# RWKV layers of a four-layer sequence: lower halves of the values read from PSUM, mixed differences of decays and gates by ACT and GpSimd in groups two to four

## The chip, the core and the metric

The kernel runs on one core of one Trainium2 chip. The time is the device time of one execution in microseconds (us); shown is the median over several runs. The engines are named as in the profile: PE (matrix multiply; PEld its weight loads), DVE (VectorE), ACT (ScalarE), POOL (GpSimd) and SP (SyncE, which here only issues transfers). Each engine works through its own queue in order.

## What is computed

Four layers run one after another on x (16 sequences x 100 steps x 512 channels, f32), each with the context ctx (16 x 361 x 512): attention (layer 0), RWKV (1), attention with a feed-forward part (2), RWKV (3). The change lies in the RWKV layers. Their first half, cut to what matters:

```python
xa = _ln(x, ln1_w, ln1_b)
sx = jnp.concatenate([state[:, 1:2] - xa[:, :1], xa[:, :-1] - xa[:, 1:]], axis=1)
xxx = jnp.tanh((xa + sx * maa_x) @ maa_w1).reshape(b, l, 5, DM)
xxx = jnp.einsum('blfd,fde->blfe', xxx, maa_w2)
xm = xa[:, :, None] + sx[:, :, None] * (maa_stack + xxx)
xk, xw, xv, xr, xg = (xm[:, :, j] for j in range(5))
w = jnp.exp(-jnp.exp(time_decay + jnp.tanh(xw @ td_w1) @ td_w2))
r, k, v = xr @ Wr.T, xk @ Wk.T, xv @ Wv.T
g = jax.nn.silu(xg @ Wg.T)
def step(s, rkvw):
    a = k_t[..., :, None] * v_t[..., None, :]
    out = jnp.einsum('bhi,bhij->bhj', r_t, u * a + s)
    s = a + w_t[..., :, None] * s
```

The five mixed inputs are numbered f = 0 (k), 1 (decay w), 2 (v), 3 (r), 4 (gate g). Each is xa + sx * (stack_f + xxx_f); `sx` is the difference of neighbouring steps.

## The kernel before

Activations lie with channels on the 128 partitions. The 512 channels are 4 chunks (NC, index c or co), the 16 sequences 4 groups (NG) of 4 sequences (G), so that one tile is 128 channels x 400 steps (T). The groups are counted from one in the text and from zero in the code: g = 0 is group one.

`rwkv` is one loop over units u, written out at build time. From u = 0 on, a unit is one pair of the 16 value columns of a chunk: 8 units a chunk, 32 a group, 128 a layer. In each unit

- `spread(u + 1)`: PE copies two value columns over the partitions into one of two PSUM pairs, `vb`. It needs the pair free, that is the scan of unit u - 1 done;
- `product(u)`: DVE writes the first state (`vb<-s`) and multiplies with k in place (`vb<-vb,kc`);
- `scan(u)`: DVE runs two scans over time into `a`; POOL multiplies `a` with r;
- in odd units `gather`: PE sums earlier products of `a`, those of units u - 3 and u - 2, into the bank `acc`.

Around this stands, as pieces of PE work with a budget for each unit, all else: the projections of the next group (`projections(g, base)`), the output of the last one, the second half of the layer. Group one is projected before u = 0, when there are no scans; groups two to four while the scans of the group before them run. The order on every engine is fixed at build time: `pin`, `mm` (L94), `turn` (L97) and the `InOrder` wrapper (L89) keep program order, so most operations show the line of the wrapper and are told apart by tile names.

The pieces use three PSUM banks in turn (`Slots`). `bank()` gives the next one, passes over one that a projection holds half done, and first emits the reader that still waits for it. `read_later` emits a reader at the end of the next unit, or as soon as its bank is asked for, or when a consumer calls it.

For one group `projections` runs through these stages:

1. layer norm, transposes, `sx`, the low-rank part `inner`;
2. the mixing stage: `repeated((0, 1))` and `mixed((0, 1), c)`, with `repeated((2, 3))` after the first chunk; for each f and chunk a matmul into a bank, then `read(f, ps)`. It writes a tile `tm` (a ring of 4, shared with others): DVE adds the column `stack{f}` to PSUM and multiplies with `sx`, POOL adds `xa` into `xj[f]`. `decay_in` follows, two matmuls for each chunk (`td_w` on xj[1], `maa_w` on xm), and first calls all readers of f = 1;
3. f = 2 and 3 with the projections k (`Wk`), and `repeated((4,))`;
4. the value stage, for each chunk c: the projection v (`plain(2, "Wv", "v", c)`), `decay(c)` (matmul with `td2`, two exponentials on ACT: `ew`, `wd`) and `mixed((4,), c)`;
5. r (`Wr`), and later the gates (`Wg`).

`plain` copies a projection on ACT into a stage tile (a ring of 6) and stores it to DRAM. For v it calls `split`: ACT rounds the bank into `hi` (the float32r upper half); DVE subtracts, `lo = v - hi`, where `v` is the stage copy in SBUF. `low` is handed to `slots.read_later` with the bank `ps`, though it reads only SBUF tiles; `enter` calls what is left of it for a chunk's loads. `hi` is stored from ACT's queue, `lo` from SP's. Both are read back for `spread`.

Of the kernel before, what the change touches and what calls it, by code (L numbers as in the profile page):

```python
# [10 lines left out]
F32R = mybir.dt.float32r  # L11
BF16 = mybir.dt.bfloat16
U8 = mybir.dt.uint8
AF = mybir.ActivationFunctionType
ALU = mybir.AluOpType
# [6 lines left out]
T = G * L  # L22
# [15 lines left out]
def xattn_sequence(ctx: ExitStack, tc: tile.TileContext, d: dict, out: bass.AP):  # L38
# [52 lines left out]
    vector, scalar, gpsimd = InOrder(nc.vector), InOrder(nc.scalar), InOrder(nc.gpsimd)  # L91

    def mm(**kw):
        pin(nc.tensor.matmul(**kw))  # L94
# [606 lines left out]
    def rwkv(n, ws, small, first, next_weights, last):  # L701
# [6 lines left out]
        with ExitStack() as es:  # L708
# [9 lines left out]
            vec, w1, td1, gwb = (small[k] for k in ("vec", "w1", "td1", "gwb"))  # L718
# [205 lines left out]
            def projections(g, base):  # L924
# [6 lines left out]
                def store(t, c, tile):  # L931
                    (nc.sync if t in ("lo", "g") else scalar).dma_start(out=to[t][c], in_=tile)

                rows = [xb[g * G + i] for i in range(G)]
                st, xn, xj = {}, [], {}
# [85 lines left out]
                def mixed(fs, c):  # L1021

                    banks = []
                    for f in fs:
                        if c == 0:
                            xj[f] = two.tile([128, NC, T], F32, tag="xm", bufs=4, name=f"xj_{nm}_{f}")
                        banks.append(slots.bank())
                    for f, ps in zip(fs, banks):
                        cols = slice(c * 128, (c + 1) * 128)
                        mm(out=ps[:, :T], lhsT=w2[f][:, cols], rhs=zs[f], start=True, stop=True)  # L1030

                    def read(f, ps):
                        tm = two.tile([128, T], F32, tag="tm", bufs=4, name=f"tm_{nm}_{f}_{c}")
                        vector.scalar_tensor_tensor(
                            tm, ps[:, :T], vec[f"stack{f}"][:, c : c + 1], st["sx"][:, c, :], ALU.add, ALU.mult
                        )
                        gpsimd.tensor_tensor(steps(xj[f][:, c, :]), steps(tm), xa(c), ALU.add)

                    for f, ps in zip(fs, banks):
                        mixes[f].append(slots.read_later(ps, lambda f=f, ps=ps: read(f, ps)))  # L1040

                def linear(f, w, co, read, tag):

                    before = mixes[f] if f >= 0 else soon
                    x = lambda c: xj[f][:, c, :] if f >= 0 else st["xm"][:, c, :]
                    chain(2.7, late, tag, before, lambda ps: ps[:, :T],
                          lambda c: w[:, c, co * 128 : (co + 1) * 128], x, read)
# [3 lines left out]
                def plain(f, w, t, co):  # L1051
                    def read(ps):
                        out = stage(f"{t}_{nm}_{co}")
                        scalar.copy(out[:, :T], ps[:, :T])
                        store(t, co, out[:, :T])
                        if t == "v":
                            split(ps, out[:, :T])

                    def split(ps, v):

                        hi = stage(f"hi_{nm}_{co}")[:, :T]
                        scalar.copy(hi.bitcast(F32R), ps[:, :T])
                        store("hi", co, hi)

                        lo = stage(f"lo_{nm}_{co}")[:, :T]

                        def low():
                            vector.tensor_tensor(lo.bitcast(F32R), v, hi, ALU.subtract)
                            store("lo", co, lo)

                        lows[co] = slots.read_later(ps, low)

                    linear(f, ws[w], co, read, ("in", g, co if t == "r" else 0))
# [362 lines left out]
            while u < UNITS + 6 or pieces or slots.due or slots.late:  # L1436
# [23 lines left out]
                elif short and len(put) == NG and blended < NG:  # L1460
                    g = blended
# [485 lines left out]
```

## Time and profile before

| | |
|---|---|
| median of 3 runs | 3131.18 us (3127.56 to 3131.5) |
| the profiled execution | 3127.86 us, of it a span of 3126.1 us |
| PE, busy share of the span | 2858.8 us, 91% |
| DVE | 1675.5 us, 54% |
| ACT | 1308.6 us, 42% |
| POOL | 1159.3 us, 37% |
| mean granted PE clock | 0.961 |
| POOL `a<-a,rc` | 256 x 1908 ns |
| DVE scans `a<-wc,vb` | 512 x 974 ns |
| POOL `xj<-tm,ext` | 160 x 981 ns |
| DVE `tm` | 160 x 625 ns (median) |
| DVE `lo` | 32, median 612 ns, sum 37.35 us |

The first RWKV layer is at work from about 690 to 1345 us of the span, the second from about 2440 us to the end. In the first, group one's values are made at 724 to 746 us, group two's at 829 to 862, group three's at 962 to 990 and group four's at 1088 to 1114; their mixing stages for f = 0 and 1 lie at 694 to 706, 788 to 807, 902 to 921 and 1030 to 1047. The second layer repeats this about 1754 us later.

The profile's views are read so. A group of instructions has a line, an engine and an operation, `out<-in` by the program's names, shapes, count, busy time, mean duration and the idle time in front of it with its releaser. A row of waits reads: engine and tile, `<-` whom it waited for, us in total, times, longest. A timeline row reads: start, length, engine, line, operation, `xcount`, and in brackets the idle time before it and the releaser; rows with a count above one are merged. A window row gives for each engine the busy time in it. Ends of matmuls are modelled, and POOL spans are rough.

### The profile page before, as it was taken

How to read it: one execution, taken by the hardware profiler on the slowest of the kernel's cores; microseconds unless marked ns; L12 is line 12 of the kernel's file. 1: busy time of each engine (PE TensorE's matmuls, PEld its weight loads, DVE VectorE, ACT ScalarE, POOL GpSimd, SP SyncE). 2: the span in 40 equal slices, each digit the busy share in tenths (PEclk: the TensorE clock that was granted, in tenths of full speed). 3: DMA queues.
4: the chain of work that ended last, by engine and by line, in shares of the span. 5: the costliest groups of instructions: out<-in, count | busy, mean ns of one | idle time of the engine just before them, and what ended most of it. 6: DMA issues, size and time to landing. Idle time of an engine off the chain costs nothing. (4 is left out here: it accounts for less than half of the span.)

```text
span 3126.1 us, 44079 instructions
## 1 busy us (share of the span) xinstructions
PE 2858.8 (91%) x16323; PEld 1488.0 (48%) x16323; DVE 1675.5 (54%) x3507; ACT 1308.6 (42%) x2921; POOL 1159.3 (37%) x953
## 2 busy tenths in 40 slices
PE   6999999878889999989999999989999789999998
PEld 3555555534344444444555555455555344444444
DVE  2555556553989988433333333331000369998981
ACT  3777677753435355422222232221111335344553
POOL 0111111133777777412222111220000367787771
PEclk9999999989999999989999999999999889999999
DMA  6010101013224353230000001020002323324321
GB/s 196 24 34 24 34 24 37 3 39 116 80 77 129 96 161 87 71 88 21 21 22 21 21 21 34 28 71 11 11 11 62 101 63 106 109 76 155 105 60 56
DMA packets 139561, 195.93 MB, mean 63 GB/s; under 512 B 23974, under 2 KB 106854, under 8 KB 139346
## 3 DMA queue, kind: packets, MB, share of 16 engines
q1 hardware_dynamic: 116306, 160.34, 17.3%
q10 hardware_dynamic: 23040, 32.78, 2.9%
q8 instruction: 128, 2.10, 0.3%
q14 instruction: 87, 0.71, 0.1%
HBM read 117.16 MB, written 49.15 MB: 53 GB/s over the span
## 5 line engine op out<-in xcount | busy, mean ns | idle before, releaser
L89 POOL TENSOR_TENSOR a<-a,rc 128x800 f32<-128x800 f32 x256 | 487.8, 1908 | 175.8 <-DVE a L89 113.1
L89 DVE TENSOR_TENSOR_SCAN a<-wc,vb 128x400 f32<-128x400 f32 x512 | 477.4, 974 | 28.1 <-PE acc L94 2.2
L89 DVE CUSTOM_DVE_ANT_0 pr<-l_sc,mask 100x361 f32<-100x361 f32 x512 | 252.1, 529 | 148.7 <-PE l_sc L94 148.6
L89 ACT ACTIVATE pr<-pr,nm 100x361 f32<-100x361 f32 x512 | 301.2, 593 | 5.8 <-POOL sums L89 3.7
L89 DVE TENSOR_TENSOR vb<-vb,kc 128x792 f32<-128x792 f32 x256 | 253.8, 991 | 8.8
L97 PEld LDWEIGHTS l_pT<-ident,pr 100*121 100x121 f32 x1536 | 193.3, 186 | 104.3 <-issue 50.9
L1639 DVE CUSTOM_DVE_ANT_0 junk<-l2a_sc,mask 100x361 f32<-100x361 f32 x256 | 136.9, 535 | 182.5 <-PE l2a_sc L94 165.0
L94 PE MATMUL vb<-xc,sel 128*128 128x400 f32 x512 | 207.0, 487 | 18.0 <-DVE a L89 17.8
L97 PE MATMUL l_pT<-ident,pr 100*121 100x100 f32 x1536 | 216.4, 276 | 6.2 <-ACT pt L89 4.3
L1675 POOL TENSOR_TENSOR pa<-pt,pt 121x1600 f32<-121x1600 f32 x16 | 57.1, 3570 | 363.7 <-ACT pt L1670 363.7
L89 ACT COPY pt<-l_pT 121x400 f32<-121x400 f32 x256 | 125.1, 489 | 149.5 <-PE l_pT L97 148.5
L1860 DVE TENSOR_TENSOR x<-pb,x 100x512 f32<-100x512 f32 x16 | 12.6, 790 | 319.9 <-DMA pb<-po 310.1
L89 POOL TENSOR_TENSOR xj<-tm,ext 128x400 f32<-128x400 f32 x160 | 153.6, 981 | 80.1 <-DVE tm L89 59.8
L94 PE MATMUL v<-l_v_w,ct 128*121 128x512 f32 x384 | 177.0, 605 | 0.0
L75 PE MATMUL h<-yTb,l_fc 128*128 128x400 f32 x512 | 172.8, 499 | 0.6 <-ACT yTb L343 0.6
L94 PE MATMUL k<-ct,l_k_w 128*128 128x361 f32 x512 | 170.6, 476 | 0.0
L75 PE MATMUL p<-l_proj,h 128*128 128x512 f32 x384 | 165.5, 592 | 0.0
L89 POOL TENSOR_SCALAR ve<-mv 100x1 f32<-100x1 f32 x16 | 3.6, 224 | 409.8 <-DVE mv L89 409.8
L94 PEld LDWEIGHTS vb<-xc,sel 128*128 128x128 f32 x512 | 97.2, 198 | 109.5 <-issue 36.1
L94 PE MATMUL l_sc<-kz,qz 32*100 32x361 f32 x1024 | 112.6, 509 | 36.1 <-DVE nm L89 33.9
L89 DVE COPY pt<-l_pT 121x400 f32<-121x400 f32 x128 | 73.5, 574 | 132.1 <-PE l_pT L97 64.8
L75 PEld LDWEIGHTS h<-yTb,l_fc 128*128 128x128 f32 x512 | 96.9, 190 | 74.3 <-ACT yTb L343 2.5
(298 smaller groups left out, 5158.0 us busy)
## 6 DMA issues: line engine op xcount, KB each, us to landing
ct<-in_ctxT SPq DMA_DIRECT2D x32, 722.0 KB
dk<-k ACTq DMA_DIRECT2D x32, 200.0 KB
kc<-dk SPq DMA_DIRECT2D x32, 200.0 KB
dv<-v ACTq DMA_DIRECT2D x32, 200.0 KB
dhi<-hi ACTq DMA_DIRECT2D x32, 200.0 KB
dlo<-lo SPq DMA_DIRECT2D x32, 200.0 KB
vc<-dv SPq DMA_DIRECT2D x32, 200.0 KB
dw<-wd ACTq DMA_DIRECT2D x32, 200.0 KB
```

The lines of the kernel that those rows point to most:

```text
L75: nc.tensor.matmul(out=ps, lhsT=lhs(c), rhs=rhs(c), start=(c == 0), stop=(c == n - 1))
L89: return lambda *args, **kw: tc.keep_in_program_order(op(*args, **kw))
L94: pin(nc.tensor.matmul(**kw))
L97: pin(nc.tensor.transpose(out, in_, ident))
L1639: nc.vector.tensor_tensor_reduce(out=junk, in0=ss[r][:L, :S2], in1=t["mask"], scale=-1.0, scalar=FLT_MAX, op0=ALU.add, op1=ALU.min, accum_ ...
L1675: nc.gpsimd.tensor_tensor(t["pa"], t["pt"][0], pt, ALU.add)
L1860: nc.vector.tensor_tensor(x, pb[:, i, :], x, ALU.add)
```

## The change

`read` in `mixed` splits by f and group. For f = 1 and f = 4, in groups two to four (`g` not zero), ACT adds the column to the PSUM bank and writes `tm`, POOL multiplies `tm` with `sx` in place, and POOL's add of `xa` follows as before. All other f, and all of group one, stay with DVE. There are 4 chunks x 2 f x 3 groups x 2 layers = 48 such reads of 160.

`split` no longer gets the copy `v`. DVE computes `lo` from the bank itself, 32 times, in all groups.

```diff
                     def read(f, ps):
                         tm = two.tile([128, T], F32, tag="tm", bufs=4, name=f"tm_{nm}_{f}_{c}")
-                        vector.scalar_tensor_tensor(
-                            tm, ps[:, :T], vec[f"stack{f}"][:, c : c + 1], st["sx"][:, c, :], ALU.add, ALU.mult
-                        )
+                        if f in (1, 4) and g:
+                            scalar.activation(tm, ps[:, :T], AF.Identity, bias=vec[f"stack{f}"][:, c : c + 1], scale=1.0)
+                            gpsimd.tensor_tensor(tm, tm, st["sx"][:, c, :], ALU.mult)
+                        else:
+                            vector.scalar_tensor_tensor(
+                                tm, ps[:, :T], vec[f"stack{f}"][:, c : c + 1], st["sx"][:, c, :], ALU.add, ALU.mult
+                            )
                         gpsimd.tensor_tensor(steps(xj[f][:, c, :]), steps(tm), xa(c), ALU.add)
...
                         if t == "v":
-                            split(ps, out[:, :T])
+                            split(ps)
-                    def split(ps, v):
+                    def split(ps):
...
                         def low():
-                            vector.tensor_tensor(lo.bitcast(F32R), v, hi, ALU.subtract)
+                            vector.tensor_tensor(lo.bitcast(F32R), ps[:, :T], hi, ALU.subtract)
                             store("lo", co, lo)
```

No buffer, bank or piece is added, and PE's order is the same.

## The prediction

> **What bounds the kernel now.** The page first: PE is busy 91% of the span, DVE 54%, and in the two RWKV layers (690 to 1345 us and 2440 to 3126 us) both are near full. I then asked for the first RWKV layer in stretches cut by stage. Columns: length, then busy us of PE, PEld, DVE, ACT, POOL with instruction counts, granted clock, DMA.
>
> ```profile
> 755.00:828.00 73.00, 60.71 (x240) 29.49 (x238) 57.34 (x85) 23.32 (x40) 51.10 (x42) 0.86 0.21 60
> 828.00:866.00 38.00, 32.87 (x128) 15.36 (x124) 36.80 (x45) 24.38 (x47) 27.89 (x22) 1.00 0.41 134
> 962.00:996.00 34.00, 31.41 (x124) 14.78 (x122) 31.48 (x43) 24.65 (x48) 24.21 (x19) 1.00 0.53 170
> 1026.00:1060.00 34.00, 29.97 (x118) 13.73 (x116) 30.84 (x48) 9.91 (x17) 26.82 (x21) 0.80 0.26 73
> ```
>
> Rows 2 and 3 are where groups two and three make their values (Wv): DVE 97% and 93%, PE 86% and 92%. Row 4 is the mixed-difference stage of group four (row 1 holds group two's): POOL already 79%, and a clock below 1. No engine alone sets the pace: the chain of waits over 2500 to 2960 us has PE's mm at 34.4%, DVE's scans and products at 20.3%, DVE tm at 2.5%, DVE lo at 1.3%. So work taken off DVE pays only where DVE is last. Next, the two tiles that the change touches, and PE's waits over the whole run (us, times, longest):
>
> ```profile
> L89 DVE TENSOR_TENSOR lo<-v,hi x32: 549/612/3915, 728.1 to 2867.2; 128x400 fp32r<-128x400 f32 x32
> L89 DVE SCALAR_TENSOR_TENSOR tm<-mm,vec,sx x160: 607/625/635, 697.8 to 2863.7; 128x400 f32<-128x400 f32 x160
> L89 DVE TENSOR_TENSOR rk<-mm,vc x32: 548/549/575, 773.4 to 3013.4; 128x400 f32<-128x400 f32 x32
> ...
> PE mm L94 <- DVE tm L89: 18.7, 26, 1.8
> PE mm L94 <- ACT hi L89: 11.4, 13, 2.3
> PE mm L94 <- POOL xj L89: 4.5, 5, 1.4
> ```
>
> lo, with both inputs in SBUF, stretches up to 3915 ns; tm and rk, with one input in PSUM, never stretch. In the timeline the long ones lie over POOL's products:
>
> ```profile
> 859.11 3.92 DVE L89 TENSOR_TENSOR lo<-v,hi 128x400 fp32r<-128x400 f32 x1
> 859.72 1.88 POOL L89 TENSOR_TENSOR a<-a,rc 128x800 f32<-128x800 f32 x1
> ```
>
> **Part 1: lo from PSUM.** The 32 lo take 37.35 us (four windows, 2.30 + 16.25 + 2.30 + 16.50). At rk's 0.549 us, the same shape with PSUM and SBUF inputs, they take 17.6: 19.8 us less DVE work, nearly all in groups two and three. The PSUM row (549) is no slower than the quickest lo from SBUF (549), so I charge nothing for the source.
>
> [...]
>
> The move also adds a wait. lo now reads the PSUM bank, so PE's next matmul there waits for DVE's lo, not only for ACT's hi. With three banks taken in turn, the next taker is the next Wv group or the decay/gate mixing matmul before it. Group one shows the plainest case:
>
> ```profile
> 728.12 0.58 DVE L89 TENSOR_TENSOR lo<-v,hi 128x400 fp32r<-128x400 f32 x1 [6.21 <-ACT hi L89]
> 728.14 2.95 PE L94 MATMUL mm<-xj,l_Wv 128*128 128x400 f32 x8 [0.23 <-ACT hi L89]
> ```
>
> PE starts as hi ends; afterwards it starts after lo, 0.58 later, four times a layer (728, 733, 740, 745) with DVE idle: at most 2.3 us, and half of that where PE would have waited for ACT's ew anyway. I take +1.2 a layer.
>
> In groups two to four I walked the rows bank by bank. At 836.57 the mixing matmul follows hi (835.82); afterwards it waits for the scan (ends 837.13), rk (0.55) and lo (0.55): 838.2, 1.6 late, and behind it in PE's queue stand Wv (0.85 late) and a spread whose product is a unit off. At 857.94 Wr takes the bank of the last value: it must wait for the scan's end (859.19) and lo, about 2 us. Against this DVE gains 3.35 us on the lo at 859 and 0.62 on each tm. Both advances meet: DVE often catches up with ACT's hi and then waits for it, ACT in turn for the late PE. By the walk PE is 1.1 us ahead at 870 (group two, where "PE waits for DVE rk" shrinks), 0.2 ahead at 996, 0.2 behind at 1118: -1.1 a layer.
>
> **Part 2: tm of decays (f = 1) and gates (f = 4).** 4 chunks x 2 x 3 groups x 2 layers = 48. DVE loses 48 x 0.625 = 30 us. ACT gains 48 x about 0.59 (the row of ew, an activation with a bias from PSUM) = 28 us; ACT is busy 10 to 24 us of 34 to 38 in these stages, so this is hidden, except where its queue holds two table loads (845.4 to 848.6) ahead of a gate's tm: there decay's bank, freed by DVE at 848.7, comes about 1 us later. That is in the walk. Cover gone, it would be 48 x 0.59. POOL gains 48 multiplies; none of this shape on tm exists, but its flat 128x400 product (rk, 1.04 us) is the same form: 50 us, half in the mixing stage, where four multiplies come within three units. What is queued behind them: POOL's own adds to xj, then the next product a, for which PE's gather waits.
>
> The stage of group four shows the queue:
>
> ```profile
> 1041.19 1.88 POOL L89 TENSOR_TENSOR a<-a,rc 128x800 f32<-128x800 f32 x1 [0.43 <-DVE a L89]
> 1043.03 2.80 POOL L89 TENSOR_TENSOR xj<-tm,ext 128x400 f32<-128x400 f32 x3
> 1045.88 0.55 PE L94 MATMUL mm<-xj,td_w 128*64 128x400 f32 x1 [0.35 <-POOL xj L89]
> 1047.37 0.17 DVE L89 COPY vb<-s 128x8 f32<-128x8 f32 x1 [1.67 <-PE vb L94]
> ```
>
> POOL goes almost without a pause from 1036.1, and PE's decay matmul already waits for its last add. With two more multiplies by 1041.8 (one ahead of a, 0.6 late) and two among the three adds, that add ends near 1048.6: +2.75 us, and DVE behind it is waiting for PE already, so nothing hides it. Group two (POOL busy 791 to 802, PE waiting at 799.56) comes out 0.9 late; group three, whose decay chunk three starts 2.4 us after its add, 0.8. Together +4.4 a layer. Bounds: 0 if the earlier release of banks by ACT pays for it all, 4 x 1.04 = 4.2 in each of three groups (12.5) if none hides.
>
> **Sum.** A layer: +1.2 - 1.1 + 4.4 = +4.5; two layers +9.0. On the profiled execution (3127.86 us, a span of 3126.1 and 1.8 around it) this gives 3136.9. That execution lies 3.3 below the median of the runs (3131.18), and the forecast for the median is 3131.2 + 9, rounded to 3140.
>
> Ends: if only the gains reach the end, the chain gives them: its three lo in 2500 to 2960 us (0.89 + 3.84 + 1.13 = 5.86) shrink to 1.65, and tm's 2.5% of 460 us, 24/80 of it, is 3.5: -7.7 a layer, -15. If POOL hides nothing: 2 x (12.5 + 2.3) = +30.
>
> The clock is a further unknown. At 905 to 919 us it fell to half after PE gaps of at most 1.4 us, and matmuls of td_w took 0.87 to 0.93 instead of 0.50. So new waits of 1 to 2.75 us could cost clock too: 12 us at half clock hold 6 us of lost work. Equally, banks freed earlier could end a slow stretch sooner by as much. I take 0.
>
> [...]
>
> **Rivals.** *Faster, -15 (3116).* DVE's relief (50 us of 875 us in all stages of the two layers that hold the change) reaches the end. It decides if lo is done by the time PE returns to its bank, that is if DVE stays ahead of ACT's hi, and if PE's bank waits on tm (18.7 us, of which f = 1 and 4 own 30% by count) go too. For it: DVE at 97% and 93% in the value stages. Against: there PE is fed by hi from ACT, and the bank waits come back as lo.
> *No change, within 6.* Gains and the POOL tail cancel, as all waits are 1 to 2 us in a loop where three engines wait in turn. For it: my sum is a difference of such terms.
> *Much slower, +30 (3161).* POOL becomes the bound in the mixing stages, with the full multiplies exposed in six of them. For it: 79% busy in 1026 to 1060, 91% with four more. Against: the stage ends within 10 us and POOL then has pauses of 2 to 3 us (1050.64 came after 2.88 idle).
> That lo stays stretched is unlikely: no operation with a PSUM input stretched.
>
> **How the numbers follow.** Forecast (slower, +4 to +20, own range 3135 to 3151): 0.44; much slower 0.08; no change 0.16; faster 0.32. 0.2% is 6.3 us, about what a measurement of this kernel tells from no change; slower by more 0.50, within 0.18, faster 0.32, a little of the forecast's lower edge counted as within. The range 3113 to 3156 takes in the faster case and leaves out most of the much slower one.
>
> **What will show it.** Right: lo at 0.55 everywhere; DVE busy down by some 50 us, POOL up by as much; a new PE wait on lo of 8 us or more, PE's wait on POOL xj above 4.5; decay matmuls of group four some 2.7 us later within their stage. Wrong: if PE waits on lo stay under 3 us and the value stages shorten by 2 us or more each, the faster case holds; if PEclk in the mixing stages rises from 0.80 and 0.86 towards 1, the clock has paid, which I put at nothing.

## The result, and the profile after

The changed kernel takes 3159.81 us (median of 6 runs, 3153.92 to 3166.76), beside 3130.31 us (6 runs, 3125.14 to 3132.42) of the kernel before on the same chip: a ratio of 1.0099, 95% interval [1.0085, 1.0114], that is +31 us [+27, +36]. The forecast of +9 us had the direction; the time lies outside its range.

From here on, costs in us are (ratio - 1) times the median of the kernel before in the same series, with the interval worked out likewise. The expectations below sometimes give the difference of two medians instead (29.5 for the whole change, 15.1 for the decays alone).

The profiled execution took 3153.92 us, of it a span of 3152.1. The page's first part, busy time of each engine:

```profile
PE 2862.7 (91%) x16323; PEld 1493.6 (47%) x16323; DVE 1633.1 (52%) x3459; ACT 1334.6 (42%) x2969; POOL 1205.4 (38%) x1001
```

DVE lost 42 us of work, ACT got 26, POOL 46: the work moved as meant. The changed operations, by tile (shortest, median and longest duration in ns):

```profile
L89 DVE TENSOR_TENSOR lo<-mm,hi x32: 549/575/576, 725.7 to 2894.3; 128x400 fp32r<-128x400 f32 x32
...
L89 ACT ACTIVATE tm<-mm,vec x48: 573/594/610, 792.6 to 2891.0; 128x400 f32<-128x400 f32 x48
L89 POOL TENSOR_TENSOR tm<-tm,sx x48: 1024/1034/1049, 794.4 to 2894.8; 128x400 f32<-128x400 f32 x48
```

No lo stretches any more, and the prices taken from other rows (0.55, 0.59 and 1.04 us) hold within 0.03. What went wrong is not there but in what waits for these operations. PE's waits, the same view as before (total, times, longest):

```profile
PE mm L94 <- DVE lo L89: 27.9, 24, 2.5
PE mm L94 <- POOL xj L89: 26.2, 15, 3.8
...
PE mm L94 <- ACT tm L89: 12.2, 11, 1.5
...
PE mm L94 <- DVE tm L89: 6.2, 12, 0.8
```

PE stands 27.9 us at banks for lo, where it stood 11.4 for hi, and 26.2 instead of 4.5 us for POOL's xj.

To see where the time was lost, one DVE operation served as a mark: the 32 starts of rk, one for each chunk of scans. Marks 0, 4 and 8 of a layer stand ahead of the mixing stages of groups two, three and four, and the next mark behind each. The table gives how much each stretch between marks grew against the kernel before, in both layers: "mixing stages" sums the stretches 0 to 1, 4 to 5 and 8 to 9, "value stages" the rest up to the next group (1 to 4, 5 to 8, 9 to 12). (The expectations call such marks anchors and cut the stages a little differently.)

| kernel | against before, us | mixing stages | value stages |
|---|---|---|---|
| whole change | +31.0 [26.6, 35.7] | +17.7 | +7.7 |
| lo alone | +6.3 [2.5, 9.7] | +1.3 | +2.8 |
| tm alone (f = 1 and 4) | +19.4 [15.3, 23.5] | +18.2 | +2.9 |
| decays alone (f = 1) | +16.3 [11.3, 21.3] | +18.5 | -7.6 |
| gates alone (f = 4) | +4.4 [0.6, 7.8] | -1.3 | +5.9 |
| lo and gates | +14.4 [9.1, 19.7] | -0.2 | +17.6 |
| POOL's multiplies alone | +13.5 [9.4, 17.5] | +15.5 | -1.6 |
| decays, PE's waits filled | +5.3 [2.5, 8.1] | +11.9 | -4.6 |
| whole change, waits filled | +22.2 [16.9, 27.5] | +11.5 | +7.6 |
| before, two waits filled | +2.5 [-1.3, 5.9] | +3.0 | -2.0 |
| gates of group two alone | -3.4 [-7.8, 0.6] | +0.9 | +8.3 |

The last two columns come from one execution each, and executions of one kernel differ by 10 us and more (3121.61 to 3135.02 for the kernel before in one series). The last two kernels of the table, which take the time of the kernel before, show what that does. In the mixing stages they differ from it by 3 us at most, so that column can be read. In the value stages they differ by -2.0 and +8.3 us. The execution of before that serves as the yardstick was slow in one of these stages (group two, second layer: every kernel of the table came out 1.1 to 5.3 us shorter). And the last kernel leaves group three as it was, yet its stretches grew by 3.9 and 2.8 us in the two layers. So what stands firm is that whatever moves the decays loses 15 to 18 us in the mixing stages (12 with the waits filled). In the value stages only the +17.6 of lo and gates stands out; for the rest the times of the kernels decide, and that lo and the gates cost there follows from where their operations stand.

### The profile page after: what moved, and what is told of

It is laid out like the page before. It is cut to its first block, busy times and chain, and to the rows that moved or that the text cites. A ratio compares the mean times of both kernels' runs of the same rounds, so it can differ in the third digit from the quotient of the medians.

```text
span 3152.1 us, 44127 instructions
## 1 busy us (share of the span) xinstructions
PE 2862.7 (91%) x16323; PEld 1493.6 (47%) x16323; DVE 1633.1 (52%) x3459; ACT 1334.6 (42%) x2969; POOL 1205.4 (38%) x1001
```

## The experiments

**The parts one by one.** Four kernels: lo from PSUM with every tm on DVE; tm as changed with `lo = v - hi`; and the latter for one f only.

```diff
-                        if f in (1, 4) and g:
+                        if f == 1 and g:      # decays alone; f == 4: gates alone
...
-                            vector.tensor_tensor(lo.bitcast(F32R), ps[:, :T], hi, ALU.subtract)
+                            vector.tensor_tensor(lo.bitcast(F32R), v, hi, ALU.subtract)
```

> Part 1 alone: lo read from PSUM, every tm left with DVE. The whole change cost 29.5 us, by anchors in the trace about half in the mixing stages of f = 0 and 1 (+1.0, +2.3, +3.7 a layer) and half in the value stages (+1.5, +4.9, 0). Theory A (two causes: POOL's queue in the mixing stages, and in the value stages the gate's tm behind ACT's table loads, which makes hi and lo late): this kernel costs little, 0 to +5 us, and the mixing stages do not move. Rival B (PE waiting at its banks for lo is the main cost): +15 us or more. Rival C (the lo from PSUM gains what it saves of DVE, 20 us of busy time): -5 us or less. PE's waits on lo stay above 8 us in sum under A and B.

> Part 2 alone: tm of f = 1 and 4 in groups two to four by ACT and POOL, lo = v - hi from SBUF as before. Theory A: +20 to +30 us, nearly all of the change's cost. Rival B (lo's bank wait is the main cost): +5 to +14 us, the mixing stages' share alone. Rival C: as much as or more than the whole change (29.5 us), because lo stretches again over more POOL work.

> Only the decays' tm (f = 1) by ACT and POOL in groups two to four, the gates' tm with DVE, lo from SBUF. Theory A: +12 to +16 us (two layers times the +7.0 that the anchors show in the mixing stages), with PE's waits on POOL xj near 20 us. Rival (the mixing stage's delay is caught up in the stage behind it, where PE waits for DVE): within 5 us of before. Rival B and C make no statement of it.

> Only the gates' tm (f = 4) by ACT and POOL in groups two to four, the decays' tm with DVE, lo from SBUF. Theory A: +8 to +14 us, all in the value stages, with ACT's tm behind the loads of its tables and hi, lo and Wr late. Rival B: within 3 us of before, because without lo's wait at the bank ACT's lateness is hidden.

Measured: +6.3, +19.4, +16.3 and +4.4 us. The decays carry half of the change, and lo alone, which was meant to gain, costs too (PE waits 33.4 us for it). Theory A holds for the decays, is within the interval for lo (0 to +5 forecast) and puts the gates too high (+8 to +14); rivals B (lo above 15) and C (lo gains) fall. The parts add up to 27.0 us, and the intervals don't tell that from 31.0.

**Why the decays are dear: POOL, ACT or the ring?** First, DVE keeps tm, and POOL gets the same extra multiply into xj, which its add then overwrites:

```diff
+                        if f == 1 and g:
+                            gpsimd.tensor_tensor(xj[f][:, c, :], tm, st["sx"][:, c, :], ALU.mult)
                         gpsimd.tensor_tensor(steps(xj[f][:, c, :]), steps(tm), xa(c), ALU.add)
```

> The kernel before, with one more POOL multiply of 128x400 for each tm of f = 1 in groups two to four (tm times sx, written to xj, where POOL's add overwrites it), ahead of that add; DVE makes tm as before. It adds the POOL work of the decays' multiplies alone. Theory A (POOL's queue ahead of the last add): +12 to +18 us, PE's wait on xj near 25 us in sum. Rival C (ACT's part of the chain): within 5 us of before.

Measured: +13.5 us. Nothing else was changed, so POOL's work alone brings most of the decays' 16.3. PE's wait for xj in this run:

```profile
PE mm L94 <- POOL xj L89: 19.5, 10, 3.2
```

Second, all three steps in place in xj, without a tile of the ring:

```diff
-                            scalar.activation(tm, ps[:, :T], AF.Identity, bias=..., scale=1.0)
+                            tm = xj[f][:, c, :]
+                            scalar.activation(tm, ps[:, :T], AF.Identity, bias=..., scale=1.0)
```

> f = 1 by ACT and POOL in groups two to four as in the run with the decays alone, but all three steps work in place in xj, so that ACT needs no tile of the tm ring. In that run ACT waited for POOL's xj to give back a tm tile 4 times, 8.2 us, in the first RWKV layer. Theory A (POOL's work itself): +11 to +18 us, as with the ring. Rival (the ring: ACT held up, hence the bank, hence PE): +6 us or less.

Measured: +13.5 us [9.4, 17.8]; the ring is not it. Third, ACT adds the column in the bank and DVE multiplies:

```diff
+                            scalar.activation(ps[:, :T], ps[:, :T], AF.Identity, bias=..., scale=1.0)
+                            vector.tensor_tensor(tm, ps[:, :T], st["sx"][:, c, :], ALU.mult)
```

> For f = 1 in groups two to four ACT adds the column in place in the PSUM bank and DVE multiplies the bank with sx into tm; POOL has its add alone, as before. It adds the ACT operation and its latency without the POOL work. Theory A: -2 to +5 us, PE's wait on xj under 8 us. Rival C (ACT late as the first reader of the bank): +10 us or more.

Measured: +8.1 us [4.4, 12.2], between the two. Here the bank comes free only after ACT and DVE in turn, which neither kernel has: PE's wait for DVE's tm rose from 18.7 to 26.5 us, that for xj was 7.0 (4.5 before). It says that an ACT step put in front has a price of its own; it does not split the 16.3. Fourth, DVE makes the last add in POOL's place:

```diff
+                            gpsimd.tensor_tensor(tm, tm, st["sx"][:, c, :], ALU.mult)
+                            vector.tensor_tensor(steps(xj[f][:, c, :]), steps(tm), xa(c), ALU.add)
```

> f = 1 in groups two to four: ACT adds the column, POOL multiplies with sx, and DVE adds xa into xj. POOL has one operation for each chunk as in the kernel before, DVE one too; only who does which is exchanged, and the chain from bank to xj has the same three links as in the run with the decays alone (+15.1 us). Theory A (the amount of POOL work in the mixing stage): 0 to +7 us, PE's wait for POOL on xj gone. Rival C (the longer chain ACT, POOL, third operation is late, whoever does it): +12 us or more. DVE's add has both inputs in SBUF and may stretch over POOL's products, which would put some of it back.

Measured: +54.8 us [49.7, 60.1], far above what theory A allows; rival C's "+12 or more" takes in the number, but not by a late chain for PE, whose wait for POOL's xj fell to 2.0 us. The cost is not in DVE's add (median 0.575 us) but in DVE's queue: DVE waited 64.0 us, 22 times, for POOL's tm with the scans behind it. As a test of POOL's load it fails; it shows what a consumer of POOL costs on the engine that paces the scans.

**The clock behind the waits.** In the run with the decays alone, PE's timeline in the mixing stage of group three, second layer, reads (start, length, idle time before and its releaser):

```profile
2676.98 0.55 PE L94 MATMUL mm<-xj,td_w 128*64 128x400 f32 x1 [1.86 <-POOL xj L89]
...
2679.93 0.93 PE L94 MATMUL mm<-xj,td_w 128*64 128x400 f32 x1 [2.05 <-POOL xj L89]
...
2680.64 0.87 PE L94 MATMUL mm<-xj,td_w 128*64 128x400 f32 x1
...
2683.81 5.28 PE L94 MATMUL mm<-xj,l_Wk 128*128 128x400 f32 x8
```

After the second wait everything takes nearly twice as long: td_w 0.93 instead of 0.55, eight Wk 5.28 instead of 2.85. So PE was kept busy in these waits, in groups three and four, by matmuls with a zero weight that add zero to the bank:

```diff
                         for c in (2 * i, 2 * i + 1):
+                            for _ in range({2: (0, 2, 2, 2), 3: (0, 0, 4, 2)}.get(g, (0, 0, 0, 0))[c]):
+                                mm(out=ps[:64, :T], lhsT=zero, rhs=st["xm"][:, c, :], start=False, stop=False)
```

> The decays alone by ACT and POOL (+15.1 us), and in groups three and four PE gets matmuls with a zero weight (100 lines less than the waits: 6 a group, each about 0.67 us by the rows of td_w) in front of the decay matmuls that wait for POOL's xj; they add zero to the bank. If the half clock that follows those waits (td_w 0.93 and 0.87 instead of 0.50, Wk x8 5.28 instead of 2.85 us in the second layer's group three) is a part of the cost: the rows behind the filled waits run at 0.50 and 2.85, and the time falls to +6 to +12 us. Rival (the clock is only a companion, POOL's queue sets the time): +15 us within 3, whether the clock stays or not.

(The first parenthesis should say that the six a group are a little shorter than the waits.) The same stage then reads:

```profile
2672.21 0.55 PE L94 MATMUL mm<-xj,td_w 128*64 128x400 f32 x1 [0.36 <-POOL xj L89]
...
2675.16 0.55 PE L94 MATMUL mm<-xj,td_w 128*64 128x400 f32 x1 [0.72 <-POOL xj L89]
...
2677.83 2.85 PE L94 MATMUL mm<-xj,l_Wk 128*128 128x400 f32 x8
```

Measured: +5.3 us [2.5, 8.1] instead of +16.3 [11.3, 21.3]. PE's idle waits for xj fell from 26.0 to 10.4 us, but the 24 zero matmuls take some 24 x 0.67 = 16 (0.67 by the rows of td_w): PE is held up at POOL's xj about as long as in the run with the decays alone, partly at work for nothing. Still 11 us, give or take 6, are gone, and td_w and Wk are back at 0.55 and 2.85 us, with a granted clock of 0.90 instead of 0.74 in this stage (2657 to 2688 us): these 11 us were the clock. With the fill in the whole change:

> The whole change, with PE's zero-weight matmuls in front of the waiting decay matmuls of groups three and four as in the run with the decays alone and filled waits (which came to +5 us instead of +15). If the half clock behind the POOL waits carries 10 us of the cost, whatever else is changed: +18 to +22 us against before. Rival (the other parts of the change take up what the clock gives): +27 us or more. Second rival (the mixing stages were the root of the value stages' loss too): +15 us or less.

Measured: +22.2 us instead of +31.0; the intervals overlap, but the 9 us agree with the 11, and the marks show the gain where the fill stands (mixing stages +17.7 to +11.5).

The kernel before has half clock too (0.51 granted from 905 to 919 us), after waits of 1.39 (group three) and 1.63 us (group four) in the first matmuls of the mixing stages. Group three, first layer:

```profile
901.77 0.44 PE L94 MATMUL mm<-zh,copies 32*128 32x400 f32 x1 [1.39 <-DVE g L89]
...
913.55 0.93 PE L94 MATMUL mm<-xj,td_w 128*64 128x400 f32 x1 [0.67 <-DVE tm L89]
```

Two zero matmuls were put into each of these waits:

```diff
                         for f, ps in zip(fs, banks):
+                            for _ in range(2 if (g, i, f) == (3, 1, 1) else 0):
+                                mm(out=ps[:64, :T], lhsT=zero, rhs=st["xm"][:, 0, :], start=False, stop=False)
                             mm(out=ps[:, :T], lhsT=copies[rs, i, :], rhs=z[i][rs], start=(i == 0), stop=(i == 1))
+                            for _ in range(2 if (g, i, f) == (2, 0, 0) else 0):
+                                mm(out=ps[:64, :T], lhsT=zero, rhs=st["xm"][:, 0, :], start=False, stop=False)
```

> The kernel before, with two zero-weight matmuls on PE in each of the two waits after which its clock falls in the mixing stages of groups three (1.39 us, for DVE's g) and four (1.63 us). Their rows there are at half clock for some 12 us each (td_w 0.87 to 0.93 instead of 0.50). If those drops cost time: -4 to -10 us. Rival (POOL's last add sets the end of these stages, so that a faster PE only waits longer): within 4 us of before.

Measured: ratio 1.0008 [0.9996, 1.0019]. In group three the clock fell all the same: the granted clock of the stage is 0.76 in the first layer, as before, and 0.78 instead of 0.83 in the second. In group four it rose, in stretches of 28 and 34 us, from 0.76 to 0.88 and from 0.86 to 1.00, and the stage there grew by 0.3 and 0.0 us by the marks. PE waited longer instead, over the whole run 7.4 us for xj (4.5 before) and 22.8 for DVE's tm (18.7). So in the kernel before the half clock of group four is free: others than PE set the end of that stage. For group three the run decides nothing.

**The value stages: lo and the gates.** Both together, without the decays:

> lo read from PSUM in all groups and the gates' tm by ACT and POOL in groups two to four; the decays' tm stay with DVE. Alone they cost +6 and +4. If their costs add: +8 to +12 us. If they meet in the value stages (the gate's tm behind ACT's table loads makes hi late, lo waits for hi, PE for lo at its bank): +14 to +20 us, with PE's waits on lo no shorter than the 27.9 us of the whole change. By the whole change less the decays one would expect 31 - 15 = 16.

Measured: +14.4 us [9.1, 19.7], against 6.3 + 4.4 = 10.7: the intervals don't tell a sum from an interaction. The rows show a chain. ACT in group three's value stage, second layer, of this run:

```profile
2746.15 1.28 ACT L89 ACT_TABLE_LOAD   x1 [0.39 <-ACT wd L89]
...
2748.06 1.28 ACT L89 ACT_TABLE_LOAD   x1
2749.35 0.54 ACT L89 ACTIVATE sq<-sq 128x400 f32<-128x400 f32 x1
2749.79 0.58 ACT L89 ACTIVATE tm<-mm,vec 128x400 f32<-128x400 f32 x1
2750.27 0.48 ACT L89 COPY v<-mm 128x400 f32<-128x400 f32 x1
...
2751.15 0.49 ACT L89 CAST hi<-mm 128x400 fp32r<-128x400 f32 x1 [0.40 <-ACT v L89]
```

DVE and PE at the same place:

```profile
2751.68 0.57 DVE L89 TENSOR_TENSOR lo<-mm,hi 128x400 fp32r<-128x400 f32 x1 [3.77 <-ACT hi L89]
```

```profile
2750.42 0.45 PE L94 MATMUL mm<-zs,w 128*128 128x400 f32 x1 [0.99 <-ACT tm L89]
2752.30 2.28 PE L94 MATMUL mm<-xj,l_Wr 128*128 128x400 f32 x4 [1.43 <-DVE lo L89]
2753.78 1.47 PE L94 MATMUL vb<-xc,sel 128*128 128x400 f32 x2
```

The gate's tm stands behind two table loads; with it v, hi, lo and the first Wr matmul, which takes the value's bank, come late, and behind the two waits PE runs at half clock (vb 1.47 instead of 0.83, Wr x4 2.28 instead of 1.61, the next of either in this run). DVE, which the move was to relieve, stands idle for 3.77 us. Two kernels cut one link each. The first leaves the tm behind the loads (4 of 24) with DVE:

```diff
-                        if f == 4 and g:
+                        if f == 4 and g and (g, c) not in ((1, 1), (2, 2)):
```

> As the run with lo and gates together (+14.4 us), but the one gate's tm of group two (chunk two) and the one of group three (chunk three) that stand behind two loads of ACT's tables stay with DVE: 4 of 24. If the loads are what makes the gates' move dear (tm, then v, hi, lo, then Wr late, and half clock behind it: 5.1 and 4.2 us in group three's value stages by the anchors): +5 to +9 us. Rival (lo's wait at the bank and ACT's load in general): +12 to +17 us.

Measured: +6.6 us [2.8, 10.0], no more than lo alone and 7.8 less, give or take 6, than lo and gates together. So these four reads carry much of the price of the gates, perhaps all of it. PE's waits for ACT's tm fell from 5.9 to 0.9 us. The rest of the chain is not borne out: PE waits for lo as long as with lo and gates together (31.6 us, 31.0 there), and the first Wr matmul, second layer, still waits and still runs slow:

```profile
2748.68 2.43 PE L94 MATMUL mm<-xj,l_Wr 128*128 128x400 f32 x4 [2.01 <-DVE lo L89]
```

The marks don't help: group three's stages lost 1.8 and 2.7 us instead of 4.5 and 3.7, less than untouched stages move. Through which of its links the table loads cost the 7.8 us stays open. The second kernel takes only the last chunk's lo from the copy in SBUF, in the whole change:

```diff
-                            vector.tensor_tensor(lo.bitcast(F32R), ps[:, :T], hi, ALU.subtract)
+                            vector.tensor_tensor(lo.bitcast(F32R), v if co == 3 else ps[:, :T], hi, ALU.subtract)
```

> The whole change (+29.5 us), but lo of the last chunk of each group (8 of 32) is read from the SBUF copy again, so that PE's first Wr matmul, which takes the bank of that value, waits for ACT's hi alone. In the whole change group three's value stages lost 4.9 and 3.6 us by the anchors, with a wait of 1.43 us for lo there and half clock behind it. If that wait is the cause: group three's value stages lose under 2 us each, no half clock in Wr, and the time comes to +20 to +25 us. Rival (hi itself is late, behind the gate's tm and the table loads, and PE waits for it as long): the value stages stay above 3 us and the time at +27 us or more.

Measured: +24.1 us [19.1, 29.1], 6.9 less, give or take 7, than the whole change. The first Wr matmuls of group three wait 0.82 us for ACT's hi in place of 1.43 for lo and stay at full clock (x4 1.61). By the marks its stage lost 2.3 us in the first layer instead of 3.7, and 5.8 instead of 4.1 in the second, again no more than untouched stages move; "under 2 us each" is not met. In the second layer another wait for a lo came up earlier, and the clock fell there. PE's timeline:

```profile
2747.30 0.70 PE L94 MATMUL mm<-zs,w 128*128 128x400 f32 x1 [2.40 <-DVE lo L89]
2747.79 2.87 PE L94 MATMUL mm<-xj,l_Wv 128*128 128x400 f32 x4
```

So the wait at that bank is probably one cause, and not the only one. How much of the price of lo and gates is the clock was not measured: no run fills these waits. Could DVE serve lo sooner? In the kernel with lo alone, low was put right behind hi:

```diff
-                        lows[co] = slots.read_later(ps, low)
+                        low()
+                        lows[co] = lambda: None
```

> lo read from PSUM as in the run with part 1 alone (+6 us, PE waits on lo 33.4 us in sum), but DVE's lo is put right behind ACT's hi in program order, not at the end of the next unit; all tm with DVE. If PE waits because lo stands behind a scan and a product in DVE's queue: PE's waits on lo fall below 15 us and the time comes to within 3 us of before, or below it. Rival (DVE now stands at lo until ACT has rounded hi, with the scans behind it): +8 us or more, with DVE's wait for ACT's hi well above the 74 us of the whole change.

Measured: +38.8 us [33.2, 44.4], the rival. PE's wait for lo fell to 11.5 us as hoped, but DVE stands at lo with the scans behind it; its wait for ACT's hi, 66.4 us with lo alone and 74.1 in the whole change, became

```profile
DVE lo L89 <- ACT hi L89: 111.9, 30, 7.1
```

**A version that beats both?** Three tries: the gates of group two alone; these with the two filled waits of the kernel before; these with lo from PSUM in group two.

> Only the gates' tm of group two (f = 4, four chunks a layer) by ACT and POOL; groups three and four as before, lo from SBUF. By the anchors in the trace of the run with all gates moved, group two's stages gained 3.3 and 2.8 us and groups three and four lost 4.1 and 6.4 in the two layers. If that reading holds: -3 to -8 us against before. Rival (the anchors show the scatter of one execution, or the groups' effects are not independent): within 3 us of before.

> The filled waits of the run before this one, and the gates' tm of group two by ACT and POOL (measured alone at ratio 0.9989). If both gains are real and independent: -5 to -12 us. Rival (neither is): within 4 us of before.

> lo from PSUM and the gates' tm by ACT and POOL in group two alone; groups one, three and four and all decays as before. Group two is where lo from SBUF had stretched to 3.9 us and where DVE was busiest (97%). If DVE's relief is worth something there: -4 to -8 us. Rival (lo's wait at the bank takes it back): within 4 us of before.

Measured: ratios 0.9989 [0.9975, 1.0002], 0.9997 [0.9987, 1.0008] and 1.0005 [0.9994, 1.0017]. None can be told from the kernel before. The gain of 3 to 8 us that the marks seemed to promise for group two is not confirmed (the first interval, -7.8 to +0.6 us, does not rule out a smaller one); it came from marks that move as much in untouched stages.

## Why the prediction was wrong, point by point

- **"lo at 0.55 everywhere", "DVE busy down by some 50 us, POOL up by as much"**: right in kind (0.549 to 0.576; -42 and +46). lo from PSUM was no slower than the unstretched one from SBUF (0.549 us the shortest of each), as the rows had it.
- **Group one, +1.2 a layer**: right in the first layer only. From the Wv matmuls at 723.82 us to the first Wr at 744.57 PE took 20.75 us before, and from 721.43 to 743.16, 21.73 us after: +1.0. In the second layer the same stretch took 21.37 us before and 21.32 after.
- **"I take 0" for the clock**: the step that failed most. Filling the waits took 11 us of the decays' 16.3 and 9 of the whole change's 31. The text had seen that gaps of at most 1.4 us came ahead of half clock and that the new waits would be 1 to 2.75 us long, and then set gain against loss. The waits were new and on PE's path; only the loss was to be had. The sign that it named, a granted clock that rises in the mixing stages, did not come: 0.80 again in group four's of the first layer (1034 to 1068 us) and 0.84 instead of 0.86 in group two's (755 to 831). The share of half clock in these stages hardly changed; but by the filled waits it now costs time, which in group four of the kernel before it did not.
- **The mixing stages, +4.4 a layer**: the queue was read rightly, its price not. Group four's last add was forecast 2.75 us late. In the whole change POOL ran there without a pause, the timeline of POOL and then of PE:

```profile
1051.50 1.03 POOL L89 TENSOR_TENSOR tm<-tm,sx 128x400 f32<-128x400 f32 x1
1052.61 1.88 POOL L89 TENSOR_TENSOR xj<-tm,ext 128x400 f32<-128x400 f32 x2
1054.45 1.03 POOL L89 TENSOR_TENSOR tm<-tm,sx 128x400 f32<-128x400 f32 x1
1055.56 0.96 POOL L89 TENSOR_TENSOR xj<-tm,ext 128x400 f32<-128x400 f32 x1
```

```profile
1053.62 0.55 PE L94 MATMUL mm<-xj,td_w 128*64 128x400 f32 x1 [3.84 <-POOL xj L89]
...
1056.57 0.93 PE L94 MATMUL mm<-xj,td_w 128*64 128x400 f32 x1 [1.84 <-POOL xj L89]
...
1057.29 0.87 PE L94 MATMUL mm<-xj,td_w 128*64 128x400 f32 x1
```

  The marks give 3.8 us for group four in each layer, 1.0 and 1.7 for group two (0.9 forecast), but 2.3 and 5.1 for group three, where 0.8 was forecast: 17.7 in both layers, twice the 8.8. With the waits filled, which leaves mostly POOL's lateness, the decays cost 5.3 [2.5, 8.1]. So 8.8 was, if anything, too much for the queue alone, and what was missing is the clock behind it.
- **Value stages, -1.1 a layer**: the sign failed. The walk along the banks foresaw PE's wait for lo (8 us or more; it was 27.9), but let DVE's shorter lo pay for it. DVE's gain can't be spent while DVE waits for hi, and its waits for hi grew from 46.1 to 74.1 us. The gates' tm behind the table loads was named, at "about 1 us"; PE waited 1.5 us for it in group two and 0.99 in group three, and the clock after it was again not counted. lo and gates together cost +14.4 where the forecast had 2 x (1.2 - 1.1) = +0.2.
- **The rivals**: the time came out at the much slower one's +30, but not by its mechanism. POOL's multiplies exposed give +13.5, and by the filled waits of the decays much of that may be clock, though this kernel was not run with filled waits. By the times the 31 us are about 5 of POOL's lateness, 11 of the clock behind it and 14 of lo and gates, each within some 6 us. The faster rival's condition, that lo is done when PE returns to its bank, was not met (24 waits). 0.08 for the much slower case was too little: its +30 was the sum with nothing hidden, and had left out the clock.

## What to carry to other kernels

An engine that is busy at 37% over all, as POOL was, can be full in the stage that an edit touches (79% from 1026 to 1060 us before; 6.69 of 6.85 us from 1049.67 us after): count an added operation there, against the consumer of the last one in the stage, and ask what the consumer's clock does during its wait. Here two waits of 1.86 and 2.05 us on PE cost nearly as much again in the half clock behind them (8.6 us from the td_w at 2679.93 us to the vb behind Wk, 5.0 with the waits filled); zero matmuls in the wait are a cheap test of that share. And moving a read to PSUM, or an operation to another engine, moves the release of the bank too (PE waited 27.9 us for lo): look at what that engine has in its queue just ahead, table loads among it (two of 1.28 us here), before counting what the old engine saves.

## What the runs showed of the hardware

- No one length of wait explains when the clock fell in these runs. It fell after single idle waits of 2.01 us (lo and gates without those behind the table loads: Wr x4 2.43), 2.40 us (shown above: zs 0.70 and Wv x4 2.87, where 0.45 and 1.50 are full) and 3.84 us (whole change: td_w 0.55, then 0.70), and not after one of 1.57 us (lo alone: Wr x4 1.61); but neither after 2.29 us (lo and gates, 2737.16 us: Wv x4 1.50), nor after 2.25 us in the kernel before:

```profile
2606.29 0.45 PE L94 MATMUL mm<-zs,w 128*128 128x400 f32 x1 [2.25 <-ACT hi L89]
2606.58 1.50 PE L94 MATMUL mm<-xj,l_Wv 128*128 128x400 f32 x4
```

  After a wait of 1.86 us td_w took 0.55 us with the decays alone, and 0.78, then 0.87, in group three of the whole change (920.86 us). Behind the filled waits, with 0.36 to 1.21 us of idle time left, td_w stayed at 0.55.
- Behind zero-weight matmuls in the waits td_w took 0.55 instead of 0.93 us, and the mean granted clock of the decays alone rose from 0.958 to 0.964 over all runs. In the kernel before it rose from 0.961 or 0.962 to 0.963, without a gain in time; there group three stayed at 0.76 in the first layer with two of them in its wait.
- One SBUF input replaced by PSUM removed every stretch of lo under POOL's products (3915 ns before, 576 at most after). With the last chunk's lo back in SBUF its eight had a median of 1102 ns.
